# The order of GpSimd's work where a decoder's first attention ends: ternary weight pieces and context rotation

## The chip, the cores and the metric

The kernel runs on one core of a Trainium2 chip. A core has engines that each work through their own queue of instructions in order: TensorE (PE; matmuls and transposes), VectorE (DVE), ScalarE (ACT) and GpSimd (POOL) for elementwise work, and SyncE (SP), which issues most transfers (DMAs). An instruction waits at the head of its engine's queue until what it needs is there, and everything behind it waits too. The metric is device time in microseconds (us) of one execution, less is better.

## The reference, cut to what matters

Two decoder layers work on `x` (8 x 112 tokens of 512) and a context (8 x 375 of 128), each as attention, cross attention, feed-forward. Everything is fp32. The change lies where the first layer's attention passes into its cross attention, and touches three parts of what is computed:

```python
# layer 0, attention: rotated queries, softmax with one extra "sink" column
q = q * cos + _rotate_half(q) * sin
combined = jnp.concatenate([scores, sink_col], axis=-1)
probs = jax.nn.softmax(combined, axis=-1)[..., :-1]
out = jnp.einsum('bhqk,bhkd->bhqd', probs, v)
# layer 0, cross attention: the context is rotated too
kv_rope = kv_c * cos[None] + _rotate_half(kv_c) * sin[None]
# layer 0, feed-forward: weights become signs
def ternarize_weights(w):
    gamma = jnp.mean(jnp.abs(w))
    return jnp.sign(jnp.round(w / (gamma + EPS))) * gamma
```

## The kernel before, in words

**The first attention** runs in eight turns (g, hf): four groups of heads, and in each the two halves of the batch (four batches each). Turn 7 is (3, 1), so its tiles are called `p_3_1_0` to `p_3_1_3` and so on. For a turn one key tile `kT` and four query tiles `qT` are prepared by `roped` (L475 to L484): TensorE projects (`pr_k`, `pr_q`), ScalarE copies the result out of PSUM with the bias (`raw`, L475), SP moves its halves into `turned` with four DMAs (L480), GpSimd multiplies `raw` by the cosine (L482), VectorE multiplies `turned` by the sine (L483), and GpSimd adds both into `qT` or `kT` (L484). Then four units, one for each batch, are scored: `ps` = `qT` against `kT` (L528, four query tiles in turn, so the scores need all four). `softmax` follows: GpSimd copies the sink column into the probability tile `p` (L347), VectorE adds the mask (L349) and takes the maximum (L352), ScalarE does eight exponentials (L355), VectorE the reciprocal (L358), GpSimd the product with it (L359). `p` has three buffers. TensorE then transposes `p` (`ppt`, L370), VectorE copies that to `pT` (L371), TensorE multiplies by `v` (`po`, L544), and ScalarE keeps the result in `oT` (L549). Finished rows are projected (`po_at`, L235) and VectorE adds them to `x` (L335). L235 is the line of the helper that issues every accumulated matmul.

**The handover.** While turn 6 runs, turn 7 is prepared; ahead of its keys and queries stand the "early" steps of the cross attention (`context_steps`): the eight context blocks `kv` are loaded by SP, the first rows of each are transposed (`pctx`), and each block is rotated by `rope`: two products on GpSimd into a tile `by` with two buffers (L653, L654; in the profile `ctxr`), then two operations on VectorE that change `kv` in place (L655, L656). In turn 7 the rest of the first attention is woven with transposes of `kv` (`pkv`, L789, copied by ScalarE to `kvT`), the layer normalization of the new `x`, and the first fold of the cross attention's weights (`pB`, `pV`, `pR`). The cross attention begins with its queries `pq_x`.

**The ternary pieces.** The first feed-forward's weights, 32 pieces of 128 x 512, are turned into signs by `ternary_piece`, called in the cross attention's turns: GpSimd issues the load `tr` (L866), compares with both bounds (L867, L868), subtracts (L869), and issues the store into a scratch in DRAM (L870). Both tiles come from the same two `by` buffers, so a piece's load cannot start before the previous piece's subtraction. The signs are read back later, by GpSimd's queue, at L903 (`sign_fc`) and L1019 (`sign_proj`).

**What sets the order.** TensorE's order in the attention is fixed by hand (`weave` mixes a main list of steps with fillers by their costs). VectorE, ScalarE and GpSimd are ordered by a scheduler, which takes an instruction when it believes that its inputs are ready. `tc.issue_after(i)` forces the instructions inside it to stand behind instruction `i` in that order. Before the change, only the load of a piece has such a constraint: it stands behind `last[0]`, the last rope product on GpSimd.

Of the kernel before, what the change touches and what calls it, by code (L numbers as in the profile page):

```python
# [12 lines left out]
ALU = mybir.AluOpType  # L13
# [3 lines left out]
NB, T, D = 8, 112, 512  # L17
# [74 lines left out]
def _spans(widths):  # L92
    at, out = 0, {}
    for k, n in widths.items():
        out[k] = (at, n)
        at += n
    return out, at
# [58 lines left out]
def decoder(ctx: ExitStack, tc: tile.TileContext, i: dict, out: bass.AP):  # L156
    nc = tc.nc
# [8 lines left out]
    def stage_pool(name, side="left"):  # L166

        return tc.alloc_tile_pool(name=name, bufs=2, side=side, reuse_waits="tile")
# [4 lines left out]
    def fetch(out, src, behind=None):  # L173

        if behind is None:
            with tc.issue_after(issued[-1]) if issued else nullcontext():
                issued.append(nc.sync.dma_start(out=out, in_=src).ins)
        else:
            engine, last = behind
            with tc.issue_after(last):  # L180
                engine.dma_start(out=out, in_=src)
# [11 lines left out]
    spans, n = _spans(_COLS)  # L193
# [7 lines left out]
    rspans, n = _spans(_ROWS)  # L201
# [3 lines left out]
    def const(name, parts=P):  # L205
        at, n = _CONSTS[name]
        return consts[:parts, at : at + n]
# [22 lines left out]
    def turning(name):  # L230
        return psum.tile([P, D], F32, tag="t", name=name)
# [58 lines left out]
    def turned_tile(src, xT, k, name):  # L290

        pt = turning(f"pt_{name}_{k}").rearrange("p (c t) -> p c t", c=NC)
        for c in range(NC):
            nc.tensor.transpose(pt[:, c, :], src[:, c * P : (c + 1) * P], ident)
        for hf in range(2):
            lo, hi = max(k * P, hf * HT), min((k + 1) * P, (hf + 1) * HT)
            if lo < hi:
                nc.scalar.copy(xT[hf][:, :, lo - hf * HT : hi - hf * HT], pt[:, :, lo - k * P : hi - k * P])  # L298
# [20 lines left out]
    def entering(pool, xT, name, tiles, bufs):  # L319
# [5 lines left out]

        return [(0.0, norm)] + [(0.45, lambda k=k: turned_tile(xn[k], xT, k, name)) for k in tiles]


    GROUPS = [[0, 1, 2], [3], [4, 5], [6]]

# [10 lines left out]
    def softmax(pool, ps, mask, sinks, name):  # L341

        n = T if sinks is None else T + 1
        p = pool.tile([T, 8, n], F32, tag="p", bufs=3, name=f"p_{name}")
        src = ps[:T, :, :T]
        if sinks is not None:
            nc.gpsimd.tensor_copy(p[:, :, T], sinks)  # L347
        if mask is not None:
            nc.vector.tensor_tensor(p[:, :, :T], src, mask.unsqueeze(1).to_broadcast([T, 8, T]), ALU.add)  # L349
            src = p  # L350
        nmax = spool.tile([T, 8], F32, tag="nmax", name=f"nmax_{name}")
        nc.vector.tensor_reduce(nmax, src, AX.X, ALU.max, negate=True)  # L352
        total = spool.tile([T, 8], F32, tag="total", name=f"total_{name}")
        for h in range(8):
            nc.scalar.activation(  # L355
                p[:, h, :], src[:, h, :], AF.Exp, bias=nmax[:, h : h + 1], accum_out=total[:, h : h + 1]
            )
        nc.vector.reciprocal(total, total)  # L358
        nc.gpsimd.tensor_tensor(p[:, :, :T], p[:, :, :T], total.unsqueeze(2).to_broadcast([T, 8, T]), ALU.mult)  # L359
        return p  # L360

    def probs_transposed(pool, p, kept, name):
# [44 lines left out]
    def self_attention(layer, following=None, behind=None, xT=None):  # L407
# [112 lines left out]
        def scores(n, u):  # L520
            g, hf = turns[n]
            nm = f"{layer}_{g}_{hf}_{u}"
            kT, qT = held[n]["kT"], held[n]["qT"]
            ps = wide(f"ps_{nm}").rearrange("p a (h k) -> p (a h) k", h=4)
            for h in range(4):
                for k, (b, s) in enumerate(parts(n, u)):
                    at = slice(s * width, (s + 1) * width)
                    nc.tensor.matmul(  # L528
                        ps[:T, 4 * k + h, :T], qT[at, h, bcols(b)], kT[at, bcols(b)], start=True, stop=True
                    )  # L530
            held[n]["p", u] = softmax(
                mid, ps, const("mask0", T) if l0 else None, row("sinks")[:, 8 * g : 8 * g + 8] if l0 else None, nm
            )
# [98 lines left out]
        q = [(1.7, lambda c=c: queries(c)) for c in (0, 2)]  # L632
        return [(2.5, rank), v[0], v[1], *q, v[2], v[3]]

    def context_steps(pool, kv, last):


        cosk = const("coskv", LC).rearrange("p (c d) -> p c d", c=NLC)
        sink = const("sinkv", LC).rearrange("p (c d) -> p c d", c=NLC)
        hd = DCTX // 2  # L640
        for b in range(NB):
            fetch(kv[:, b], i["ctx"][b].rearrange("(c p) d -> p c d", p=LC))

        def raw(b0):
            pt = turning(f"pctx_{b0}").rearrange("p (b t) -> p b t", b=4)
            for b in range(b0, b0 + 4):
                nc.tensor.transpose(pt[:, b - b0, :T], kv[:T, b, 0, :], ident[:T, :T])
            nc.scalar.copy(ctxT[:, b0 : b0 + 4, :], pt[:, :, :T])

        def rope(b):  # L650
            by = pool.tile([P, D], F32, tag="by", name=f"ctxr_{b}")[:LC, : NLC * DCTX]
            by = by.rearrange("p (c d) -> p c d", c=NLC)
            nc.gpsimd.tensor_tensor(by[:, :, :hd], kv[:, b, :, hd:], sink[:, :, :hd], ALU.mult)  # L653
            last[:] = [nc.gpsimd.tensor_tensor(by[:, :, hd:], kv[:, b, :, :hd], sink[:, :, hd:], ALU.mult).ins]  # L654
            nc.vector.tensor_tensor(kv[:, b], kv[:, b], cosk, ALU.mult)  # L655
            nc.vector.tensor_tensor(kv[:, b], kv[:, b], by, ALU.add)  # L656

        return [(0.45, lambda b=b: raw(b)) for b in (0, 4)] + [(0.0, lambda b=b: rope(b)) for b in range(NB)]

    def cross_attention_0():  # L660

        vpool = stage_pool("xa0v", "right")
        pool = epool = kpool = kvT = xT = None
        kv = vpool.tile([LC, NB, NLC, DCTX], F32, tag="kv", bufs=1, name="kv")
        oT, last = [], []
        folds = [{} for _ in range(G)]

        turns = [(g, hf) for g in range(G) for hf in range(2)]
# [112 lines left out]
        def extra(n):  # L781
            if not 0 <= n < 7:
                return []
            return [(0.0, lambda k=k: ternary_piece(vpool, k, last[0])) for k in range(5 * n, min(5 * n + 5, 32))]

        def turn_context(b):
            pt = turning(f"pkv_{b}")
# [28 lines left out]
        def go():  # L816
            nonlocal pool
            pool = stage_pool("xa0")
            ffn = []

            def finale(outs):
                epool.release()
                kpool.release()
                ffn.append(ffn_0())
                return ffn[0]["finale"](outs)

            pipeline(
                turns, HB, 1, prepared, lambda n, u: scores(n, batches(n)[u]),
                lambda n, u: contexts(n, batches(n)[u]), outputs, extra, begun=True, finale=finale,
            )  # L830
            pool.release()
            ffn[0]["go"](vpool)

        return {"early": context_steps(vpool, kv, last), "finale": first_finale, "go": go}

# [23 lines left out]
    def ternary_piece(pool, k, behind):  # L861

        m, at = k // 16, slice(k % 4 * D, (k % 4 + 1) * D)
        w, low = (pool.tile([P, D], F32, tag="by", name=f"{t}_{k}") for t in ("tr", "tl"))
        with tc.issue_after(behind):
            nc.gpsimd.dma_start(out=w, in_=i["c_w"][k // 4][:, at])  # L866
        nc.gpsimd.tensor_scalar(low, w, down[:, m : m + 1], None, ALU.is_lt)  # L867
        nc.gpsimd.tensor_scalar(w, w, up[:, m : m + 1], None, ALU.is_gt)  # L868
        nc.gpsimd.tensor_tensor(low, w, low, ALU.subtract)  # L869
        nc.gpsimd.dma_start(out=scratch[k // 4][:, at], in_=low)  # L870
# [180 lines left out]
    def cross_attention_1():  # L1051
        with (
# [41 lines left out]
            def scores(n, u):  # L1094
                b, nm = n * HB + u // 2, f"e_{n}_{u}"
                ps = wide(f"ps_{nm}").rearrange("p a (h k) -> p (a h) k", h=4)
                for c in range(4):
                    for k in range(2):
                        at = slice(64 * (u % 2) + 32 * k, 64 * (u % 2) + 32 * k + 32)
                        nc.tensor.matmul(  # L1100
                            ps[:T, 4 * k + c, :T], held[n]["qT"][at, c, bcols(b)], held[n]["kT"][at, c, bcols(b)],
                            start=True, stop=True,
                        )
                held[n]["p", u] = softmax(pool, ps, const("mask1", T), None, nm)
# [184 lines left out]
    with tc.manual_schedule(engines={mybir.EngineType.PE}):  # L1289
        self_attention(0, cross_attention_0)[1]()  # L1290
# [22 lines left out]
```

## Time and profile before

| | us |
|---|---|
| median of 3 runs | 2024.25 (2022.91 to 2027.71) |
| the profiled execution | 2024.79 |
| its span, first to last instruction | 2022.8 |
| turn 7's first scores (L528), first to last matmul | 374.86 to 393.0 |
| first ternary load on GpSimd | 355.40 |
| last ternary store on GpSimd | 685.09 |
| first query of the cross attention (`pq_x`) | 470.11 |
| read-back of the first signs issued (L903) | 820.94 |

In the timelines a row gives start and length in us, engine, line and operation, output tile and input tiles, shape and count; in brackets stands how long the engine was idle before it, and which engine and tile released it. The busy rows of the page cut the span into 40 slices of 50.6 us, each digit being tenths of a slice.

### The profile page before, as it was taken

What the parts mean: (1) busy time and instruction counts of PE and PEld (TensorE: products, weight loads), DVE (VectorE), ACT (ScalarE), POOL (GpSimd) and SP (SyncE); (2) the same over time, 40 slices, a digit from 0 to 9 for tenths busy, and PEclk for the clock granted to TensorE, in tenths of its full rate; (3) what the DMA queues carried; (4) which work ended last, traced back from release to release, by engine and by line L of the source; (5) the groups of instructions that cost most, each with busy time, mean ns of one, the idle gap of its engine ahead of it and who ended that gap; (6) DMA issues with size and microseconds to landing.
All of it is one profiled execution on the core that took longest, in us unless ns stands there. A gap on an engine that the chain in (4) does not pass through costs nothing.

```text
span 2022.8 us, 19697 instructions
## 1 busy us (share of the span) xinstructions
PE 1891.7 (94%) x7096; PEld 1016.6 (50%) x7096; DVE 792.4 (39%) x1380; ACT 643.8 (32%) x1926; POOL 583.0 (29%) x526
## 2 busy tenths in 40 slices
PE   6899998588999999999999999998889999999999
PEld 3444444244545454457765555555554444454444
DVE  3455555333545353586632233345641021211113
ACT  2334433143433333365422232335522111121210
POOL 2444445765555300000024435302221111010111
PEclk9999999788999999999999999998889999989999
DMA  5032322423323100211121222300020000000000
GB/s 218 23 106 66 110 76 53 144 54 121 107 57 108 43 0 1 83 67 38 63 65 37 74 67 44 127 31 22 1 100 0 0 0 0 0 0 0 0 0 37
DMA packets 35455, 108.64 MB, mean 54 GB/s; under 512 B 6623, under 2 KB 19991, under 8 KB 28702
## 3 DMA queue, kind: packets, MB, share of 16 engines
q1 hardware_dynamic: 28222, 77.93, 11.9%
q0 software_dynamic: 6848, 29.36, 5.0%
q8 instruction: 56, 0.92, 0.2%
q14 instruction: 41, 0.34, 0.1%
q10 hardware_dynamic: 288, 0.09, 0.0%
HBM read 78.79 MB, written 10.22 MB: 44 GB/s over the span
## 4 chain that ended last, share of the span: by engine, by line
PE 70%; DVE 5%; ACT 3%; POOL 2%; DMA 2%; issue 1%; SPq 0%; ACTq 0%; DVEq 0%; POOLq 0%
PE pf L235 15%; PE po L235 10%; PE po_at L235 5%; PE pr_q L235 5%; PE po_x L235 5%; PE po_x L748 3%; PE pq_x L235 3%; PE po_ff L984 2%; PE ph L235 2%; PE ps_x L714 2%; PE pk_x L694 2%; PE ppt_x L739 2%; PE po L544 1%; DMA tr<-in_c_w_dram 1%; PE pv L235 1%; PE po_e L235 1%
## 5 line engine op out<-in xcount | busy, mean ns | idle before, releaser
L235 PE MATMUL po_at<-wo,oT 128*128 128x512 f32 x448 | 209.4, 615 | 3.3 <-ACT raw_q L475 3.3
L235 PE MATMUL pf<-xT_ff,fup 128*128 128x448 f32 x512 | 203.6, 552 | 2.2 <-ACT xT_ff L298 1.6
L235 PE MATMUL pr_q<-xT_at,wq 128*128 128x448 f32 x512 | 204.8, 545 | 0.0
L235 PE MATMUL po<-fdn,h 128*128 128x512 f32 x448 | 198.4, 595 | 0.0
L1237 POOL TENSOR_TENSOR h<-silu,h 128x448 f32<-128x448 f32 x64 | 72.3, 1131 | 430.2 <-ACT silu L1236 430.2
L235 PEld LDWEIGHTS pf<-xT_ff,fup 128*128 128x128 f32 x512 | 99.2, 195 | 100.4 <-issue 94.0
L355 ACT ACTIVATE p<-p,nmax 112x113 f32<-112x113 f32 x256 | 95.8, 376 | 137.1 <-DVE nmax L352 137.1
L235 PEld LDWEIGHTS pr_q<-xT_at,wq 128*128 128x128 f32 x512 | 94.5, 191 | 86.2 <-issue 78.3
L235 PEld LDWEIGHTS po<-fdn,h 128*128 128x128 f32 x448 | 83.8, 190 | 106.3 <-issue 106.2
L359 POOL TENSOR_TENSOR p<-p,total 112x896 f32<-112x896 f32 x48 | 81.2, 1692 | 191.3 <-DVE total L358 170.7
L235 PEld LDWEIGHTS po_at<-wo,oT 128*128 128x128 f32 x448 | 85.4, 198 | 96.2 <-issue 91.3
L1220 ACT ACTIVATE h<-pf,cols 128x448 f32<-128x448 f32 x64 | 40.5, 634 | 291.2 <-PE pf L235 291.2
L235 PE MATMUL po_x<-vo,xoT 128*128 128x512 f32 x224 | 102.0, 598 | 0.6 <-ACT xoT L752 0.6
L235 PE MATMUL pf<-h,sw 128*128 128x448 f32 x256 | 101.1, 539 | 0.0
L484 POOL TENSOR_TENSOR qT<-qT,turned_q 128x448 f32<-128x448 f32 x64 | 73.6, 1150 | 72.1 <-DVE turned_q L483 67.0
L528 PE MATMUL ps<-kT,qT 64*112 64x112 f32 (+1 forms) x768 | 66.0, 280 | 27.6 <-POOL qT L484 27.1
L748 PE MATMUL po_x<-pT_x,kv 125*128 125x448 f32 x192 | 89.4, 549 | 1.6 <-ACT kr_x L695 1.4
L720 DVE TENSOR_REDUCE nmax_x<-ps_x 112x2 f32<-112x750 f32 x64 | 57.2, 933 | 83.3 <-PE ps_x L714 82.9
L528 PEld LDWEIGHTS ps<-kT,qT 64*112 64x112 f32 (+1 forms) x768 | 58.4, 186 | 57.3 <-POOL qT L484 28.7
L722 ACT ACTIVATE p_x<-ps_x,nmax_x 112x375 f32<-112x375 f32 x128 | 71.9, 574 | 45.9 <-DVE nmax_x L720 45.7
L544 PE MATMUL po<-pT,v 112*64 112x448 f32 (+1 forms) x192 | 71.3, 583 | 15.8 <-DVE pT L371 15.6
L867 POOL TENSOR_SCALAR tl<-tr,ternary_bounds 128x512 f32<-128x512 f32 x32 | 51.4, 1605 | 114.9 <-DMA tr<-in_c_w_dram 114.9
(225 smaller groups left out, 3082.3 us busy)
## 6 DMA issues: line engine op xcount, KB each, us to landing
tw<-in_c_w_dram SPq DMA_DIRECT2D x16, 512.0 KB
tr<-in_c_w_dram POOLq DMA_DIRECT2D x32, 256.0 KB, 4.3
signs<-tl POOLq DMA_DIRECT2D x32, 256.0 KB, 2.8
turned_q<-raw_q SPq DMA_DIRECT2D x128, 56.0 KB
turned_q<-raw_q SPq DMA_DIRECT2D x64, 112.0 KB
wq<-in_a_q_dram SPq DMA_DIRECT2D x4, 1024.0 KB
wo<-in_a_o_dram SPq DMA_DIRECT2D x4, 1024.0 KB
bq<-in_b_q_dram SPq DMA_DIRECT2D x4, 1024.0 KB
```

Of the source, the lines that this page charges most:

```text
L235: nc.tensor.matmul(ps, lhsT, rhs, start=(k == 0), stop=(k == len(pairs) - 1))
L355: nc.scalar.activation(p[:, h, :], src[:, h, :], AF.Exp, bias=nmax[:, h : h + 1], accum_out=total[:, h : h + 1])
L359: nc.gpsimd.tensor_tensor(p[:, :, :T], p[:, :, :T], total.unsqueeze(2).to_broadcast([T, 8, T]), ALU.mult)
L484: nc.gpsimd.tensor_tensor(dst, dst, turned, ALU.add)
L528: nc.tensor.matmul(ps[:T, 4 * k + h, :T], qT[at, h, bcols(b)], kT[at, bcols(b)], start=True, stop=True)
L544: nc.tensor.matmul(po[0 if l0 else k][at, :HT], v[:, b, kv * width : (kv + 1) * width], kept["pT"][:, 4 * k : 4 * k + 4, :].rearrange("p h ...
L720: nc.vector.tensor_reduce(nmax, ps[:T, :, :L], AX.X, ALU.max, negate=True)
L722: e = nc.scalar.activation(p[:, 2 * j + s, :], ps[:T, s, :L], AF.Exp, bias=nmax[:, s : s + 1], accum_out=total[:, 2 * j + s : 2 * j + s + 1],)
L748: nc.tensor.matmul(po[0][:, : 4 * T], kv[:, b, c, :], pTs[c], start=(c == 0), stop=(c == NLC - 1))
L867: nc.gpsimd.tensor_scalar(low, w, down[:, m : m + 1], None, ALU.is_lt)
L1220: nc.scalar.activation(at["h1"][:, c, hf * HT : (hf + 1) * HT], ps[:, :HT], AF.Identity, bias=bias)
L1237: nc.gpsimd.tensor_tensor(at["h3"][:, c, tokens], s, at["h1"][:, c, tokens], ALU.mult)
```

## The change

The softmax now remembers its latest product on GpSimd in `spread`, and two things are put behind it: the rope products stand behind the product that was the latest when the ropes were written down (that of `p_3_0_2`, the unit before), and the loads of the ternary pieces stand behind the first attention's last one (that of `p_3_1_3`) instead of behind the last rope. No operation is added or removed.

```diff
+    spread = []
...
         nc.vector.reciprocal(total, total)
-        nc.gpsimd.tensor_tensor(p[:, :, :T], p[:, :, :T], total.unsqueeze(2).to_broadcast([T, 8, T]), ALU.mult)
+        total = total.unsqueeze(2).to_broadcast([T, 8, T])
+        spread[:] = [nc.gpsimd.tensor_tensor(p[:, :, :T], p[:, :, :T], total, ALU.mult).ins]
         return p
...
-    def context_steps(pool, kv, last):
+    def context_steps(pool, kv):
...
         def rope(b):
             by = pool.tile([P, D], F32, tag="by", name=f"ctxr_{b}")[:LC, : NLC * DCTX]
             by = by.rearrange("p (c d) -> p c d", c=NLC)
-            nc.gpsimd.tensor_tensor(by[:, :, :hd], kv[:, b, :, hd:], sink[:, :, :hd], ALU.mult)
-            last[:] = [nc.gpsimd.tensor_tensor(by[:, :, hd:], kv[:, b, :, :hd], sink[:, :, hd:], ALU.mult).ins]
+            with tc.issue_after(spread[0]):
+                nc.gpsimd.tensor_tensor(by[:, :, :hd], kv[:, b, :, hd:], sink[:, :, :hd], ALU.mult)
+                nc.gpsimd.tensor_tensor(by[:, :, hd:], kv[:, b, :, :hd], sink[:, :, hd:], ALU.mult)
             nc.vector.tensor_tensor(kv[:, b], kv[:, b], cosk, ALU.mult)
             nc.vector.tensor_tensor(kv[:, b], kv[:, b], by, ALU.add)
...
-        oT, last = [], []
+        oT = []
...
-            return [(0.0, lambda k=k: ternary_piece(vpool, k, last[0])) for k in range(5 * n, min(5 * n + 5, 32))]
+            return [(0.0, lambda k=k: ternary_piece(vpool, k, spread[0])) for k in range(5 * n, min(5 * n + 5, 32))]
...
-        return {"early": context_steps(vpool, kv, last), "finale": first_finale, "go": go}
+        return {"early": context_steps(vpool, kv), "finale": first_finale, "go": go}
```

In the two built programs this changes the places of GpSimd's instructions between turn 6's last queries and the cross attention, and with them those of a few instructions of VectorE and ScalarE there. The orders of TensorE and SP are the same in both.

## Prediction

> **What bounds the kernel now.** I read the page's busy rows first, then TensorE's timeline around the first attention's end, where its busy row falls, then GpSimd's and VectorE's timelines in the same stretch.
>
> ```profile
> span 2022.8 us, 19697 instructions
> PE 1891.7 (94%) x7096; PEld 1016.6 (50%) x7096; DVE 792.4 (39%) x1380; ACT 643.8 (32%) x1926; POOL 583.0 (29%) x526
> ...
> PE   6899998588999999999999999998889999999999
> ...
> POOL 2444445765555300000024435302221111010111
> PEclk9999999788999999999999999998889999989999
> ```
>
> TensorE is busy 94% of the span, so only its idle places and its slow-clock places pay. The eighth slice of 40 (354 to 405 us) is down to half, with the clock down too, just where GpSimd is busiest. TensorE there:
>
> ```profile
> 313.80 0.84 PE L528 MATMUL ps<-kT,qT 64*112 64x112 f32 x12
> 318.29 0.72 PE L528 MATMUL ps<-kT,qT 64*112 64x112 f32 x4 [3.65 <-POOL qT L484]
> ...
> 350.48 1.76 PE L544 MATMUL po<-pT,v 112*64 112x448 f32 x2 [3.60 <-DVE pT L371]
> ...
> 364.80 5.40 PE L235 MATMUL po_at<-wo,oT 128*128 128x512 f32 x8 [3.27 <-ACT raw_q L475]
> ...
> 383.72 0.72 PE L528 MATMUL ps<-kT,qT 64*112 64x112 f32 x4 [8.20 <-POOL qT L484]
> 392.30 0.72 PE L528 MATMUL ps<-kT,qT 64*112 64x112 f32 x4 [7.86 <-POOL qT L484]
> ...
> 456.34 1.74 PE L370 MATMUL ppt<-consts,p 112*112 112x112 f32 x8 [3.67 <-POOL p L359]
> ```
>
> These six stalls add up to 30.3 us; four of them (23.4) end on GpSimd. The reader is to see the waits for `qT`, and that the matmuls after a stall are long (5.40 for eight of 128x512 against 3.61 undisturbed). GpSimd, in the same stretch:
>
> ```profile
> 316.56 0.59 POOL L653 TENSOR_TENSOR ctxr<-kv,consts 125x192 f32<-125x192 f32 x1 [5.45 <-DMA kv<-in_ctx_dram]
> 317.11 1.12 POOL L484 TENSOR_TENSOR qT<-qT,turned_q 128x448 f32<-128x448 f32 x1
> ...
> 381.85 0.54 POOL L866 DMA_DIRECT2D tr<-in_c_w_dram  x1
> ...
> 385.58 1.56 POOL L867 TENSOR_SCALAR tl<-tr,ternary_bounds 128x512 f32<-128x512 f32 x1 [1.92 <-DMA tr<-in_c_w_dram]
> ...
> 391.11 1.14 POOL L484 TENSOR_TENSOR qT<-qT,turned_q 128x448 f32<-128x448 f32 x1
> ```
>
> A `qT` add of 1.1 us stands in queue behind a rope that waits for its context, and later behind a ternary piece that waits for its load. Its own inputs had been there long before:
>
> ```profile
> 372.99 0.82 DVE L483 TENSOR_TENSOR turned_q<-turned_q,consts 128x448 f32<-128x448 f32 x1 [0.21 <-DMA turned_q<-raw_q]
> ```
>
> That is the last turned query, complete at 373.8, while its add ran at 391.1. So the queue's order cost this, not data.
>
> **What the Trainium skill says.** "TensorE: Matmul & The Clock Gate", "What's actually happening": an idle window of about 3.4 us halves TensorE's clock, and about as much sustained work restores it. The trace agrees: granted clock 0.63 in 375 to 393 us, 0.50 in 432 to 440. "SBUF — State Buffer", "Who interferes with whom": a VectorE operation with two SBUF inputs and a GpSimd operation that reads SBUF exclude each other for a whole instruction. The trace agrees in kind: around 340 to 355 us ropes took 0.58 to 0.90 us, the `kv` products 0.50 to 2.02. No page is needed for prices.
>
> **The change part by part.** Nothing is added or removed but order. In the two built programs TensorE's and SP's orders are identical; GpSimd's, and a few places of VectorE and ScalarE, differ.
>
> *Ternary pieces.* The 32 pieces (load, three operations, store) no longer start at 355.4 but behind the product of the very last softmax, `p_3_1_3`. All `qT` work and softmax products of the last turn stand ahead of them.
>
> *Ropes.* The first two leave their places ahead of and behind the last `qT` add of turn 6; all eight stand behind the product of `p_3_0_2`, mixed with `kT` and `qT` of turn 7. VectorE gets `pT_3_0_0` (both halves) ahead of most of its `kv` work, but `p_3_0_3`'s mask stays behind all sixteen `kv` operations. On ScalarE `raw_q_3_1_2` now precedes the exponentials of `p_3_0_3`.
>
> Step by step, times as in the trace:
>
> 1. The `qT` add needs the turned query ready at 312.98, so it runs at 313.1 to 314.2 and the 3.65 stall goes. From the scores at 313.80 to the end of the first `po_at` took 10.36; with plain lengths (0.97 + 0.39 + 3.54) it is 4.9. TensorE is 5.5 earlier; the next scores (334.19) come at 328.7. The context loads were issued until 322.9 and the first needed 5.6 from issue to use, so `pctx` at 329.7 is just covered; bare, it costs up to 1.
> 2. The exponentials of `p_3_0_2` ended at 340.8, now 335.3; its product runs 335.5 to 337.2, then the ropes begin.
> 3. Ropes: 16 x 0.59 = 9.4, with `kT`, two `qT` products and a `kT` add (4 x 1.13) and a copy 0.2: 14.1; two `by` buffers make them wait for VectorE about 0.6, then VectorE's last three operations 1.8: end at 353.7. Mutual exclusion with VectorE, from the lengthened rows above, I put at 1.8: 355.5. For comparison, the last six ropes with similar neighbours took 339.7 to 355.2.
> 4. TensorE meanwhile has `pT_3_0_0`'s second half about 1.5 late (3.60 before), then scores, two projections and one `po_at` without the 3.27 wait, until the second `po_at` needs the PSUM buffer of `pr_q_3_1_3`. This is what is late next: mask to 356.5, turned query 0.6, maximum 1.1, exponentials 3.1, `raw_q` 0.6: 362.1. TensorE waits there about 6.
> 5. The last turned query follows `raw_q` by 3.95 (308.40 to 312.35 in the turn before), then 0.7 on VectorE and 1.15 on GpSimd: 367.9; four score matmuls: about 369. TensorE, with a slow `po_at` of up to 5.4 from 362.2, arrives by the same time. In the trace this point is 392.95. Gain of this stage: **24**.
> 6. Up to the first cross query (470.11): `ppt`, `po_at` at 393 to 399 no longer at a slow clock after 16 us of waits: 6.2 to 4.3, **1.9**. The last two softmax maxima waited 3.1 and 1.9 for their sink copies on GpSimd; without the second, the stretch 419.2 to 431.8 shrinks by **2.3**, while the rest of its waits (ScalarE's `kvT` copies behind exponentials and table loads) stays. `pB`, `po`, `pV` after it at clock 0.50 (5.25 where later folds take 2.89): half of the excess returns, **2.4**. The `ppt` stall of 3.67 goes, as `p_3_1_3` is multiplied straight behind its reciprocal, with its slow successors (1.74 for 0.8, 5.50 for 3.54): **6.5**, of which I take 5.8. Together **12.4**.
>
> Sum 36.4. Fold loads: `ranks` was issued at 392.27, right behind the last `qT` add; it moves earlier with that, and `bq`, `bo`, `kk` follow the turned-query loads on SP to about 363, some 40 us before use.
>
> 7. The pieces then run from 404. In the trace the 23 pieces whose first comparison started from 460.15 to 680.22 lie 10.0 apart (load 4.3, three operations 4.4, issues), so 32 need 320: end at 725 to 730 instead of 685.7. The sign loads wait for pool memory at 820.94, which becomes 785: some 55 us of cover. On TensorE the pieces cost almost nothing: a turn of the cross attention with them, 594.21 to 633.15, took 38.94, without, 697.92 to 736.67, 38.75; 80 us more of that is 0.4.
>
> Profiled execution 2024.79 (span 2022.8 and 2.0 around it) less 36 gives 1988.8; the median of the runs, 2024.25, lies 0.5 lower and changes nothing.
>
> **Rivals.**
> *Ropes stay the bound longer.* If most ropes and `kv` operations run at the lengthened 0.90 and 0.95, the mask comes about 8 later: stage gain 16; with little clock returned behind, 8 instead of 12.4: gain 24, time 2001. For it: VectorE's 2.02 and 3.21 us operations in that stretch. Against: those with the longest delays stood beside a ternary load or a dense GpSimd run of `kT`.
> *Cleaner than thought.* Ropes at bare length with gaps filled, and no slow clock in the finale: TensorE alone would reach the end of the last scores at about 361, gain 32, and 13 behind: time 1980. Against: VectorE's order, which keeps the mask last.
> *Slower: the signs come late.* Place: the first `ph` matmul at 850.98, then 815; with a landing of up to 11.2 the pieces must end by 804. Each microsecond more per piece is 32. From 12.5 us a piece it eats gain; slower than before from (840 - 404) / 32 = 13.6. At 14.5 the end is 868 and the time 2053. Against: the longest distance in the trace is 12.1, the mean 10.0.
> *Nothing happens*, because a stall I give to the queue belongs to a DMA: 2024. Against: the line at 372.99.
>
> **How the numbers follow.** Forecast 0.62, slow ropes 0.20, cleaner 0.13, signs late 0.03, nothing 0.02. The forecast's own spread is about 1983 to 1996 (rope exclusion 0 to 6, clock 3). The range for 8 in 10 runs from 1979 to 2003. Faster by over 0.2% (4 us, about what a measurement of this kernel can tell from no change) 0.95, within 0.02, slower 0.03.
>
> **What would show it.** GpSimd's timeline without a piece before the last softmax product, near 404. No `qT` wait above 2 us at the last turn's scores; one wait of about 6 on `raw_q` near 355. The first cross query near 434 instead of 470, and every later stage as far apart as before. Last piece near 727, sign loads still waiting for TensorE. It is wrong if the mask of `p_3_0_3` comes after 362, or if the pieces come to meet the sign loads.

## The result and the profile after

| | before | after |
|---|---|---|
| median of the runs | 2023.58 (2022.39 to 2027.71, 4 runs) | 1993.88 (1992.84 to 1996.47, 4 runs) |
| profiled span | 2022.8 | 1992.2 |
| ratio, 95% interval | | 0.9852, 0.9834 to 0.9869 |

The change makes the kernel 1.5% faster, 29.7 us by the medians and 30.6 by the two profiled spans. The time put on record was 1988.8 with a range of 1979 to 2003. Line numbers are 2 or 3 higher in the first attention and 4 higher behind it (the scores are L531, the pieces L870 to L874).

From the page of the kernel after, TensorE's and GpSimd's busy rows and the granted clock:

```profile
span 1992.2 us, 19698 instructions
...
PE   6899999798999999989999999989899999999999
...
POOL 3444445445555530000033343312221111010111
PEclk9899999989999999999999999999789999999999
```

In the eighth slice, some 350 to 400 us, TensorE went from 5 to 7, its clock from 7 to 9, and GpSimd from 7 to 4, as the pieces left it; GpSimd's row of 5s now runs one slice longer before its empty slices begin.

The first question is whether the pieces left the last turn. GpSimd's timeline of the kernel after, at the end of the first attention:

```profile
405.78 1.68 POOL L362 TENSOR_TENSOR p<-p,total 112x896 f32<-112x896 f32 x1 [13.19 <-DVE total L360]
407.40 0.75 POOL L870 DMA_DIRECT2D tr<-in_c_w_dram  x1
410.93 1.56 POOL L871 TENSOR_SCALAR tl<-tr,ternary_bounds 128x512 f32<-128x512 f32 x1 [2.78 <-DMA tr<-in_c_w_dram]
```

The first load stands straight behind the product of the last softmax, and only now does GpSimd wait for a load. TensorE's timeline of the same kernel shows what that did (brackets: how long TensorE stood still, and for whom):

```profile
313.93 1.04 PE L531 MATMUL ps<-kT,qT 64*112 64x112 f32 x16
...
328.80 1.04 PE L531 MATMUL ps<-kT,qT 64*112 64x112 f32 x16
...
344.38 0.96 PE L547 MATMUL po<-pT,v 112*64 112x448 f32 x2 [2.71 <-DVE pT L374]
...
365.80 5.41 PE L235 MATMUL po_at<-wo,oT 128*128 128x512 f32 x8 [7.44 <-ACT raw_q L478]
...
372.05 1.23 PE L531 MATMUL ps<-kT,qT 64*112 64x112 f32 x16
373.21 0.98 PE L373 MATMUL ppt<-consts,p 112*112 112x112 f32 x8
...
406.67 5.09 PE L235 MATMUL pB<-ranks,kk 128*128 128x64 f32 x24
...
427.83 0.93 PE L373 MATMUL ppt<-consts,p 112*112 112x112 f32 x8
...
438.95 3.17 PE L235 MATMUL pq_x<-xT_xa,wr 128*128 128x448 f32 x8
```

The scores at 313.93, those at 372.05 and the transposes at 427.83 have no bracket: the waits for `qT` of 3.65, of 8.20 and 7.86, and the one of 3.67 for `p`, are gone, all of them on GpSimd's queue. The wait for `raw_q` has grown from 3.27 to 7.44, and `pB` is still slow.

Where the 30.6 us came from, by the starts of the same matmuls. In the kernel before they are these two:

```profile
392.95 1.74 PE L370 MATMUL ppt<-consts,p 112*112 112x112 f32 x8
...
470.11 3.17 PE L235 MATMUL pq_x<-xT_xa,wr 128*128 128x448 f32 x8
```

| from, to | before | after | gain |
|---|---|---|---|
| start to `ppt` behind the last turn's first scores | 392.95 | 373.21 | 19.7 |
| from there to the first `pq_x` (470.11, 438.95) | 77.16 | 65.74 | 11.4 |
| from there to the end | | | -0.6 |

The far end of the change, the pieces and the loads that read the signs back, on GpSimd's timeline of the kernel after:

```profile
728.37 0.62 POOL L874 DMA_DIRECT2D signs<-tl  x1 [0.30 <-POOL tl L873]
789.67 2.13 POOL L907 DMA_DIRECT2D sign_fc<-signs  x4 [60.67 <-PE pk_x L698]
```

The last piece is stored at 729, and GpSimd then stands 60.67 us until memory for the signs comes free. The pieces, started 52 us later than before, make nothing wait.

### The profile page after: what moved, and what is told of

It reads as the page before. It is cut to its first block, busy times and chain, and to the rows that moved or that the text cites. A ratio compares the mean times of both kernels' runs of the same rounds, so it can differ in the third digit from the quotient of the medians.

```text
span 1992.2 us, 19698 instructions
## 1 busy us (share of the span) xinstructions
PE 1881.7 (94%) x7096; PEld 1010.5 (51%) x7096; DVE 803.0 (40%) x1380; ACT 644.3 (32%) x1926; POOL 584.3 (29%) x526
## 4 chain that ended last, share of the span: by engine, by line
PE 72%; DVE 5%; ACT 4%; issue 1%; POOL 0%; DVEq 0%; ACTq 0%
PE pf L235 15%; PE po L235 11%; PE po_at L235 6%; PE pr_q L235 5%; PE po_x L235 5%; PE po_x L752 3%; PE pq_x L235 2%; PE ph L235 2%; PE po_ff L988 2%; PE ps_x L718 2%; PE pk_x L698 2%; PE ppt_x L743 2%; PE po L547 2%; PE ps L531 1%; PE pv L235 1%; PE po_e L235 1%
## 5 line engine op out<-in xcount | busy, mean ns | idle before, releaser
L547 PE MATMUL po<-pT,v 112*64 112x448 f32 (+1 forms) x192 | 70.9, 580 | 14.9 <-DVE pT L374 14.7
L485 POOL TENSOR_TENSOR qT<-raw_q,consts 128x448 f32<-128x448 f32 x64 | 74.5, 1165 | 34.1 <-ACT raw_q L476 18.5
L1254 DVE SCALAR_TENSOR_TENSOR nxt<-po,wr,nxt 128x512 f32<-128x512 f32 x42 | 31.5, 751 | 120.8 <-PE po L235 120.8
```

Of the source, the lines that this page charges most:

```text
L485: nc.gpsimd.tensor_tensor(by_batch(dst), by_batch(raw), cos, ALU.mult)
L547: nc.tensor.matmul(po[0 if l0 else k][at, :HT], v[:, b, kv * width : (kv + 1) * width], kept["pT"][:, 4 * k : 4 * k + 4, :].rearrange("p h ...
```

## The experiments

The theory: GpSimd's queue made TensorE wait, because pieces stood ahead of the last turn's query work, and ropes ahead of the turn before. Rivals: the ropes' move alone does it, or the stretch is bound by the ropes' own length.

**Pieces alone.** The ropes lose their constraint.

```diff
-            with tc.issue_after(spread[0]):
+            with nullcontext():
                 nc.gpsimd.tensor_tensor(by[:, :, :hd], kv[:, b, :, hd:], sink[:, :, :hd], ALU.mult)
```

> Only the pieces stand behind the last softmax product; the ropes are left to the scheduler as before. My theory, that nearly all of the gain is the pieces: the first two waits (3.65 and 3.60) come back, 5.5 us in all, but two ropes are done early and the sine product of 3.21 us falls to 0.6 without a load beside it, so the mask of p_3_0_3 comes near 356 (359.4 in the changed kernel) and the last turn's scores end within 2 us of the changed kernel's 373.2. Time 1991 to 1997. Rival, that the ropes' move carries the gain because it starts turn 7's chain earlier: at least 8 us slower than the changed kernel, 2002 or more.

Measured: 1993.85 (1988.76 to 1997.67), ratio 0.9862 (0.9835 to 0.9889). TensorE's timeline of this run:

```profile
350.74 1.76 PE L547 MATMUL po<-pT,v 112*64 112x448 f32 x2 [3.60 <-DVE pT L374]
...
363.54 3.70 PE L235 MATMUL po_at<-wo,oT 128*128 128x512 f32 x8 [1.42 <-ACT raw_q L478]
...
371.91 1.04 PE L531 MATMUL ps<-kT,qT 64*112 64x112 f32 x16
372.88 0.98 PE L373 MATMUL ppt<-consts,p 112*112 112x112 f32 x8
```

TensorE comes some 6 us late into this stretch (the `qT` wait of 3.50 at 318.46 and the `pT` wait of 3.60 are back), but then it waits 1.42 for `raw_q` where the changed kernel waits 7.44, and `ppt` starts at 372.88 against 373.21. What the ropes' move saves ahead of the stretch, it pays back inside it. Taking the pieces away also frees VectorE of them, but by little: the mask of `p_3_0_3` starts at 357.55, against 358.82 before, which is 1.3 us beside the 16 us of `qT` waits that went.

**Ropes alone.** The pieces stand behind the last rope again, as before the change.

```diff
-                nc.gpsimd.tensor_tensor(by[:, :, hd:], kv[:, b, :, :hd], sink[:, :, hd:], ALU.mult)
+                last[:] = [nc.gpsimd.tensor_tensor(by[:, :, hd:], kv[:, b, :, :hd], sink[:, :, hd:], ALU.mult).ins]
...
-            return [(0.0, lambda k=k: ternary_piece(vpool, k, spread[0])) for k in range(5 * n, min(5 * n + 5, 32))]
+            return [(0.0, lambda k=k: ternary_piece(vpool, k, last[0])) for k in range(5 * n, min(5 * n + 5, 32))]
```

> Only the ropes are moved; the pieces stand behind the last rope as before. My theory: the mask of p_3_0_3 comes at 359 as in the changed kernel, then the last query add stands behind two pieces and the scores end about 5 later (378 to 379); the stretch from there to the first cross query keeps its 77 us (66 in the changed kernel). Together 16 to 17 slower than the changed kernel: 2008 to 2013. Rival, ropes carry the gain: within 8 us of the changed kernel, under 2002.

Measured: 2022.7 (2013.45 to 2026.23), ratio 1.0005 (0.9992 to 1.0018): no gain, against an expected 10 to 15 us. GpSimd's timeline of this run, and below it TensorE's:

```profile
372.48 1.13 POOL L485 TENSOR_TENSOR qT<-raw_q,consts 128x448 f32<-128x448 f32 x1
378.88 1.56 POOL L871 TENSOR_SCALAR tl<-tr,ternary_bounds 128x512 f32<-128x512 f32 x1 [5.26 <-DMA tr<-in_c_w_dram]
...
384.96 1.14 POOL L487 TENSOR_TENSOR qT<-qT,turned_q 128x448 f32<-128x448 f32 x1
```

```profile
386.15 0.72 PE L531 MATMUL ps<-kT,qT 64*112 64x112 f32 x4 [12.74 <-POOL qT L487]
386.80 1.74 PE L373 MATMUL ppt<-consts,p 112*112 112x112 f32 x8
...
406.63 0.98 PE L373 MATMUL ppt<-consts,p 112*112 112x112 f32 x8 [2.54 <-POOL p L362]
...
426.78 0.89 PE L793 MATMUL pkv<-consts,kv 125*128 125x125 f32 x3 [5.27 <-DVE pT L374]
```

Between the two halves of one query's rotation stands a whole piece with its 5.26 of waiting for a load, and TensorE waits 12.74; the scores end at 386.9, not at 378 to 379. `ppt` is still 6 us earlier than before (386.80 against 392.95), but the softmax products behind it queue behind pieces as well: two waits (2.54 for `p`, and 5.27 for `pT` where the kernel before waits 2.73) take most of it back, and `pB` starts at 431.17 against 431.75. So the two parts do not add up: the pieces' move carries the gain, and the ropes' move, with or without it, is worth nothing that these runs can tell.

**No ropes.** The eight ropes are not issued.

```diff
-        return [(0.45, lambda b=b: raw(b)) for b in (0, 4)] + [(0.0, lambda b=b: rope(b)) for b in range(NB)]
+        return [(0.45, lambda b=b: raw(b)) for b in (0, 4)]
```

> The context is not rotated in the cross attention of layer 0: the ropes are left out on GpSimd and VectorE, all else as in the changed kernel. My theory, that the sixteen VectorE operations ahead of p_3_0_3's mask make what is left of the waits: the mask comes near 343 instead of 359, the 7.44 wait on raw_q and the 2.71 wait on pT go with their slow matmuls (1.8 and 0.9): 12 to 14 us less than the changed kernel, 1979 to 1983. Rival, that the wait belongs to PSUM buffers or to the turned-query transfers on SP: a wait of 5 or more stays at the second projection, and the time falls by less than 6.

Measured: 1981.34 (1979.7 to 1983.99), ratio 0.9803 (0.9782 to 0.9824). The mask of `p_3_0_3` runs at 342.78 instead of 359.44, `ppt` at 358.15 instead of 373.21. VectorE's and TensorE's lines of this run:

```profile
342.78 1.08 DVE L351 TENSOR_TENSOR p<-ps,consts 112x896 f32<-112x896 f32 x1
```

```profile
358.15 0.98 PE L373 MATMUL ppt<-consts,p 112*112 112x112 f32 x8
```

The ropes cost 15.1 us of this stage and 10 (by the ratios) to 12.5 (by the medians) of the whole: behind the change they are what is late.

**Products only.** Are GpSimd's sixteen products long, or do the two engines hold each other up? VectorE's part of the ropes is left out.

```diff
-            nc.vector.tensor_tensor(kv[:, b], kv[:, b], cosk, ALU.mult)
-            nc.vector.tensor_tensor(kv[:, b], kv[:, b], by, ALU.add)
```

> The two operations on VectorE that finish each rope are left out (kv is not changed, so the output is not the reference's); GpSimd's sixteen products stay where the changed kernel has them. Theory (the rope stretch is long because VectorE's two operations and GpSimd's products lengthen each other and share two buffers): without VectorE's part GpSimd's chain from the first product (near 337) to the last shrinks from 18.8 us to 14 to 14.7, all products take 0.55 to 0.62; the mask of p_3_0_3 comes at 342 to 344 as in the run without ropes, the last turn's scores end at 357.5 to 361, total 1981 to 1986. Rival (GpSimd's own queue is the long pole, VectorE merely follows): chain still above 17 us, scores end at 368 or later, total 1990 to 1996.

Measured: 1989.93 (1986.79 to 1991.53), ratio 0.9846 (0.9829 to 0.9862). That lies between theory and rival, and the timed runs do not tell this kernel from the changed one (0.9834 to 0.9869). The groups of instructions for the ropes (busy, then mean ns of one), first in the kernel after, then in this run:

```profile
L659 DVE TENSOR_TENSOR kv<-kv,consts 125x384 f32<-125x384 f32 x8 | 9.1, 1152 | 5.3 <-POOL ctxr L658 5.3
L660 DVE TENSOR_TENSOR kv<-kv,ctxr 125x384 f32<-125x384 f32 x8 | 7.4, 965 | 0.0
L658 POOL TENSOR_TENSOR ctxr<-kv,consts 125x192 f32<-125x192 f32 x8 | 6.7, 842 | 0.0
L657 POOL TENSOR_TENSOR ctxr<-kv,consts 125x192 f32<-125x192 f32 x8 | 5.1, 639 | 2.0 <-issue 1.5 <-POOL kT L487 0.5
```

```profile
L657 POOL TENSOR_TENSOR ctxr<-kv,consts 125x192 f32<-125x192 f32 x8 | 4.8, 597 | 0.0
L658 POOL TENSOR_TENSOR ctxr<-kv,consts 125x192 f32<-125x192 f32 x8 | 4.8, 597 | 0.0
```

Alone, every product takes 597 ns, as the theory says. The sixteen run in 8.8 us without a gap, and not in 14 to 14.7, since the `raw` products now stand behind them and not between them. But the mask of `p_3_0_3` came at 349.56, not at 342 to 344. VectorE's timeline of this run says why:

```profile
340.19 8.91 DVE L486 TENSOR_TENSOR turned_k<-turned_k,consts 128x448 f32<-128x448 f32 x1 [1.46 <-DMA turned_k<-raw_k]
349.02 0.61 DVE L486 TENSOR_TENSOR turned_q<-turned_q,consts 128x448 f32<-128x448 f32 x1
349.56 1.08 DVE L351 TENSOR_TENSOR p<-ps,consts 112x896 f32<-112x896 f32 x1
```

An operation that takes 0.62 elsewhere took 8.91. From 340.34 to 348.6 GpSimd ran thirteen operations without a gap (the last eleven products and two `raw` products), and VectorE got through beside the small copy that followed. The mask stood behind it. So a dense run of GpSimd cost VectorE's queue time although nothing needed its results.

**Ropes later.** The same ropes, written down behind turn 7's keys and queries, so that they stand behind the product of `p_3_0_3`.

```diff
-                steps = joined[0]["early"]
+                steps = joined[0]["early"][:2]
...
+            if l0 and n == 7:
+                steps += joined[0]["early"][2:]
```

> The rope steps stand behind turn 7's keys and queries instead of ahead of them, and so behind the product of p_3_0_3. My theory: p_3_0_3's mask comes near 343 and the 7.44 wait goes, but 16 ropes now stand ahead of and between the last two query adds: TensorE waits 6 to 9 for qT, and the last scores end near 365 (373.2): 1983 to 1987. Rival, that the ropes' total is what counts, wherever they stand: 1990 to 1996.

Measured: 1991.36 (1984.33 to 1993.9), ratio 0.9856 (0.983 to 0.9881). The mask comes at 342.26 and `ppt` at 366.38, 6.8 earlier than after the change, but three smaller waits are new (2.71 on `x`, 1.97 on `pT`, 1.11 on `qT`). The profiled execution is the fastest of the four, 1984.33; the median lies in the rival's range, and the timed runs do not tell this kernel from the changed one.

**Later still.** The rope steps in turn 7's fillers, behind the product of `p_3_1_1`.

```diff
+            elif n == 6:
+                steps += joined[0]["early"][2:]
...
-                steps = joined[0]["early"]
+                steps = joined[0]["early"][:2]
```

> The rope steps are written down in turn 7's fillers, so their products stand behind that of p_3_1_1. Theory (the ropes only have to be done before pkv, near 388; ahead of the scores they cost 12 to 15 us): the mask of p_3_0_3 near 342.3, the first scores of the last turn near 357, all ended near 363; the ropes then run from about 372 beside the last softmaxes, and pkv waits for the first blocks; first cross query at 425 to 432, total 1980 to 1988. Rival (the ropes only move their price: VectorE's copies pT and pkv wait for them instead): a wait of 6 us or more at pkv or pT between 375 and 405, first cross query at 433 or later, total 1990 to 1996.

Measured: 1999.13 (1995.58 to 2007.36), ratio 0.9894 (0.9868 to 0.992): no better than the changed kernel, and what the rival said of the waits came true. The last turn's first scores came early as expected (355.61), but then twelve of VectorE's sixteen operations stood ahead of one `pT` copy of the last softmaxes, and the other four ahead of the next. TensorE's timeline of this run:

```profile
385.17 1.75 PE L549 MATMUL po<-pT,v 112*64 112x448 f32 x2 [9.24 <-DVE pT L374]
389.11 1.76 PE L549 MATMUL po<-pT,v 112*64 112x448 f32 x2 [2.18 <-DVE pT L374]
```

**All on VectorE.** As the later ropes, with all four operations on VectorE, behind the reciprocal of `p_3_0_3`.

```diff
-            with tc.issue_after(spread[0]):
-                nc.gpsimd.tensor_tensor(by[:, :, :hd], kv[:, b, :, hd:], sink[:, :, :hd], ALU.mult)
+            with tc.issue_after(inverse[0]):
+                nc.vector.tensor_tensor(by[:, :, :hd], kv[:, b, :, hd:], sink[:, :, :hd], ALU.mult)
...
```

The second product is changed in the same way, and `inverse` keeps the latest reciprocal as `spread` keeps the product.

> All four operations of a rope run on VectorE, written down behind turn 7's keys and queries and put behind the reciprocal of p_3_0_3's softmax. Theory (lengthening needs both engines): where GpSimd is idle, VectorE's sums take 0.5 to 0.6 and its products 0.3 to 0.4, a block 1.5 to 1.8 and all eight 12 to 14.5 us, where the changed kernel needs 18.8; the block stands in front of the copy pT_3_0_1, which comes at 361 to 363; scores of the last turn end at 364 to 368 against 373.2, total 1983 to 1990. Rival (each operation is slow on VectorE by itself): block above 2.2 us, pT_3_0_1 after 366, total not below the changed kernel's 1992 to 1996.

Measured: 1989.66 (1985.48 to 1995.2), ratio 0.9843 (0.9821 to 0.9866). Operation times were as expected, once GpSimd's softmax product and two `raw` products were over: 0.34 for a product into `by`, 0.54 for each of the two operations on `kv`. The sequence on VectorE took longer than expected, 349.55 to 366.9, with two turned queries and a copy in it and 3.5 of holdup by GpSimd at its start; `pT` came at 365.44 (expected 361 to 363) and TensorE waited 10.06 until 367.57. The median lies at the upper edge of what the theory expected (the profiled execution, 1995.2, is the slowest of the four), and the timed runs do not tell this kernel from the changed one. The holdup works on GpSimd too. GpSimd's timeline of this run, while VectorE runs the ropes without a gap:

```profile
359.21 7.29 POOL L487 TENSOR_TENSOR qT<-qT,turned_q 128x448 f32<-128x448 f32 x1 [4.77 <-DVE turned_q L486]
```

An add that takes 1.13 elsewhere took 7.29. It ended at 366.50, just behind VectorE's `pT` copy of 365.44 to 366.05.

**The ropes in two halves**, four blocks behind `p_3_0_3` and four behind `p_3_1_1`, once on both engines and once on VectorE alone, with the changed kernel beside them.

```diff
+            elif n == 6:
+                steps += joined[0]["early"][6:]
...
-                steps = joined[0]["early"]
+                steps = joined[0]["early"][:2]
...
+            if l0 and n == 7:
+                steps += joined[0]["early"][2:6]
```

> The changed kernel itself once more, beside the two kernels below on one chip, so that they can be compared with it: 1992 to 1996 against a before near 2022.

> Ropes on GpSimd and VectorE as in the change, but four blocks written down behind turn 7's keys and queries (behind p_3_0_3's product) and four in its fillers (behind p_3_1_1's product), where pkv needs the last block only near 400. Theory (ropes cost by what is queued behind a dense run of them): the first four fit into the gap of both engines at 352 to 358, so the last turn's scores end at 359 to 364 against 373.2; the other four run from about 370 to 379 and delay a pT copy by 1 to 3; first cross query at 426 to 431, total 1982 to 1989, some 6 to 10 below the changed kernel. Rival (two stretches of ropes cost what one costs): first cross query at 433 or later, total within 4 of the changed kernel's.

> The same split with all four operations of a rope on VectorE (behind the reciprocals of the same softmaxes). Theory: a block takes 1.6 to 1.8 once GpSimd's dense products are past, four blocks 7; beside p_3_0_3's product and two raw products on GpSimd the first block is held up by about 3.5 as when all eight stood there; pT_3_0_1 at 358 to 361 and scores ended at 363 to 367; the second four 7 to 8 us from about 371; first cross query at 427 to 434, total 1983 to 1992. Rival (VectorE is too full there, GpSimd's share is needed): pT copies wait for both stretches, total above the changed kernel's.

| on the same chip | median | ratio to before, 95% |
|---|---|---|
| the changed kernel | 1995.57 | 0.9876 (0.9856 to 0.9895) |
| halves on both engines | 1993.73 | 0.986 (0.9841 to 0.9878) |
| halves on VectorE | 1988.17 | 0.9835 (0.982 to 0.9851) |

The halves on both engines miss their expectation, and the rival's holds: the scores are early (they start at 363.72), and a `pT` wait of 3.91 at 389.30 and slow matmuls take it back, with the first cross query at 436.82. The halves on VectorE are the fastest whole kernel of this study, 0.4% below the changed one; the two intervals just do not overlap, so the step is small and only just told apart. VectorE's groups on `kv` in that run:

```profile
L663 DVE TENSOR_TENSOR kv<-kv,consts 125x384 f32<-125x384 f32 x8 | 4.4, 544 | 0.0
L664 DVE TENSOR_TENSOR kv<-kv,ctxr 125x384 f32<-125x384 f32 x8 | 4.4, 544 | 0.0
```

The product and the sum on `kv` that took 1152 and 965 ns beside GpSimd's products take 544 without them.

**Longer pieces.** How far is the late end of the pieces from hurting?

```diff
         nc.gpsimd.tensor_tensor(low, w, low, ALU.subtract)
+        for _ in range(3):
+            nc.gpsimd.tensor_scalar(low, low, 1.0, None, ALU.mult)
```

> Three more operations on GpSimd in each ternary piece (a product with 1.0, results unchanged), some 1.66 us each as the piece's other operations: 32 x 3 x 1.66 = 159 us more. Theory (a cover of about 61 us lies between the last sign and its read-back on GpSimd's queue, and the queue is the only way it can hurt): 159 - 61 = 98 us come out, total 2080 to 2100, the stall at the first matmuls with signs. Rival (more cover, since the pieces need not end before the layer normalizations, or the first feed-forward reads the signs late): total below 2050; other rival (the pieces' work slows VectorE beside it): loss above 110, with the attention's stretches longer before the read-back.

Measured: 2022.16 (2017.23 to 2025.07), ratio 0.9994 (0.9982 to 1.0005), 28 above the changed kernel where 98 were expected. GpSimd's timeline of this run at the last piece, and TensorE's where the signs are first used:

```profile
837.30 0.62 POOL L876 DMA_DIRECT2D signs<-tl  x1 [0.30 <-POOL tl L875]
837.92 2.15 POOL L909 DMA_DIRECT2D sign_fc<-signs  x4
```

```profile
844.19 0.76 PE L235 MATMUL ph<-sign_fc,top_y 128*128 128x512 f32 x1 [20.13 <-DMA sign_fc<-signs]
```

The mechanism is the expected one, the read-back now follows the last store at once and TensorE waits 20.13 for it. Two sizes were wrong, and the rival with more cover had the total right (below 2050). A piece grew from 10.1 to 13.4 us, not by 5: the three added operations take 1.5 each, and two of them run while the next load is under way. And the signs were issued 48 us later, but the first `ph` started only 24.5 later (819.70 in the changed kernel): another 24 of cover lay between the read-back and its use.

## Why the prediction was right

**Mechanism.** The queue's order was the cost, as the prediction read it from one line, a turned query complete at 373.8 whose add ran at 391.1. Pieces alone give the whole gain, as far as the runs can tell, so this is shown and not only argued. What the prediction did not see is that the ropes' move adds nothing to it: its steps 1 and 2 are real, but the gain is lost in steps 3 to 5.

**Steps 1 and 2** held: scores at 328.80 (predicted 328.7), `pctx` without a wait, the product of `p_3_0_2` at 335.68 (335.5).

**Step 3** failed in one term. The bare chain was put to 353.7 and the mutual exclusion of VectorE and GpSimd at 1.8, so the last operation on `kv` should end at 355.5; it ended at 359.5. The exclusion, with what it adds to the buffer waits, is thus 5.8 and not 1.8. The traces show most of the difference: the sixteen products took 11.8 where 9.4 was put (5.1 and 6.7 in the groups above), GpSimd stood 2.0 between them where 0.6 was put, and VectorE's last three operations took 3.4 where 1.8 was put. VectorE's timeline of the kernel after, at the end of the ropes:

```profile
356.16 1.47 DVE L659 TENSOR_TENSOR kv<-kv,consts 125x384 f32<-125x384 f32 x1 [0.48 <-POOL ctxr L658]
357.56 1.96 DVE L660 TENSOR_TENSOR kv<-kv,ctxr 125x384 f32<-125x384 f32 x2
359.44 1.08 DVE L351 TENSOR_TENSOR p<-ps,consts 112x896 f32<-112x896 f32 x1
```

The product and the sums that take 0.54 each without GpSimd take 1.5 and about 1.0 here. The sixteen take 16.5 us against 8.7 where all the ropes' work is on VectorE. The prediction's own comparison pointed further than its 1.8: six ropes in 15.5 us would make 20.7 for eight (an estimate from its own rows), where step 3 put 18.3 and 22.2 was measured.

**Steps 4 and 5** follow from it: the mask ended at 360.5 (356.5), the wait on `raw_q` was 7.44 (about 6), `po_at` behind it took the slow 5.41 that was foreseen, and the last turn's scores ended at 373.3 (about 369). Stage gain 19.7 instead of 24: the missing 4.3 is the exclusion, the mis-sized term of the sum.

**Step 6** was put to 12.4 and gave 11.4, which is nearer than its parts. The first gave 1.9 as predicted, the stretch behind 419.2 shrank by 3.5 (2.3), and what hung on the `ppt` stall of 3.67 gave 6.4 (5.8). Of `pB`'s slow clock half (2.4) was to return, and in this execution nothing did (`pB` 5.09 against 5.25, the stretch with `po` and `pV` 0.35 longer). That the parts nearly balance is luck. The changed kernel's second profile shows it returning. The windows of both (columns: busy time and count of PE, PEld, DVE, ACT, POOL, then granted clock, DMA share, GB/s), first the profile after, then the second execution:

```profile
396.00:406.00 10.00, 6.51 (x38) 3.83 (x39) 6.02 (x11) 6.84 (x24) 0.22 (x1) 1.00 0.01 2
406.00:418.00 12.00, 12.00 (x45) 8.00 (x46) 2.70 (x6) 2.65 (x5) 7.72 (x7) 0.57 0.13 44
```

```profile
396.00:406.00 10.00, 8.71 (x34) 4.81 (x33) 5.13 (x10) 5.23 (x20) 0.00 (x0) 0.68 0.01 2
406.00:418.00 12.00, 11.57 (x62) 7.34 (x62) 4.22 (x10) 3.05 (x6) 7.94 (x7) 1.00 0.12 36
```

The slow clock comes in both, once over `pB` and once ahead of it, where TensorE has less to do; `pB` then takes 2.80. The program is the same, so its order does not decide this; whether the chip does is not shown. The second profile is 1987.2 us long, 5.0 shorter than the first, and 2.6 of that lie between `ppt` and the first `pq_x` (371.78 to 434.97): by it step 6 gave 14.0, so 12.4 lies between the two executions.

**Step 7** held: pieces from 407.40 (404), last store at 729 (725 to 730), read-back at 789.67 (785), cover 60.67 (55).

**Rivals.** "Signs late" was given a break-even of 13.6 us a piece; with 13.4 a piece the kernel runs at the time of before, so its place was right and its price about right. It did not come: the pieces lay 10.1 apart. Of "ropes stay the bound longer" half is true: the ropes are the bound, but by 4 us rather than 8. "It is wrong if the mask of `p_3_0_3` comes after 362" was not met (359.44).

**The sum.** The two stages were put to 36.4 and gave 31.2. Of the 5.2 between them 4.3 is the exclusion and 1.0 step 6. Behind them 0.6 was lost, where 0.4 had been put to the pieces.

## What to carry to other kernels

An engine's queue that mixes urgent short work with background work that waits for its own loads makes the urgent work wait for those loads; put the background behind the last urgent instruction, and check that its late end has cover (here 61 us on the queue, and 24 more to the first use). When two parts of a change act on the same stretch, try each alone: here one carried everything. And where VectorE and GpSimd share a chain of operations on the same memory, do not add their bare times. Here splitting the chain and giving it to VectorE alone gained 0.4%, only just told apart; neither of the two by itself, nor a later place, was shown to be better than the change.

## What the runs showed of the hardware

- A VectorE operation with both inputs in SBUF stood 8.91 us, against 0.62 elsewhere, while GpSimd ran thirteen operations without a gap. The Trainium skill ("SBUF — State Buffer", "Who interferes with whom") says that the second to issue is blocked until the first finishes. The trace agrees and goes further: here the block lasted through the whole dense run and not one instruction. It need not: in the halves on VectorE a product that takes 0.34 stood 2.93 from 347.37, and ended at 350.30, just behind the change from one of GpSimd's back-to-back operations to the next (350.04). What decides this is not shown. Copies from PSUM (`pT`, 0.62 at 338.10 in the same run) were not held up.
- It works the other way too, by fractions and by whole runs. GpSimd's products took 0.59 alone and, in the changed kernel, up to 0.97 in turns with VectorE; and in the run with all on VectorE a `qT` add stood 7.29 (1.13 elsewhere).
- Two executions of one program had the half-speed stretch of TensorE's clock at different places (0.57 over 406 to 418, or 0.68 over 396 to 406), which moved `pB` from 5.09 to 2.80. The prediction found the trace in agreement with the skill's rule that some 3.4 us of work restore the clock. Around `pB` it does not agree: in the kernel before, TensorE shows busy without a break from 430.32, and the granted clock stayed 0.50 until 440. In the kernel after, the clock fell near 407 although TensorE's last waits were only 1.33 and 1.00.
